# Four image layers with selective scans: the product with B as a TensorE matmul against a diagonal matrix, and the share of C products on GpSimd

## The chip, the cores and the metric

The kernel runs on one core of a Trainium2 chip. The metric is device microseconds of one execution, the median of three runs; lower is better. Besides, one execution was taken by the hardware profiler, and its trace is what is read here.

## The reference

The input is a batch of 4 images of 64 x 64 positions with 192 channels, fp32. Four layers follow one another, each of the form x + layer(groupnorm(x)). All four hold a selective scan over positions with 16 states per channel. Layer a runs four scans (rows and columns, forward and backward) with weights of their own over single rows or columns of 64; layer b one scan over a snake of 4,096 positions; layers c (192 channels) and d (384 channels) four scans over 4,096 positions. The core of each, cut:

```python
x_dbl = einsum('bkdl,kcd->bkcl', xs, x_proj)          # 12 + 16 + 16 rows: dt, B, C
delta = softplus(einsum('bkrl,kdr->bkdl', dts, dt_w) + bias)
A = -exp(A_logs)
def step(h, inp):
    d, bm, cm, uu = inp
    dA = exp(d[..., None] * A[None])
    dBu = (d * uu)[..., None] * bm[:, :, None, :]      # delta*x times B
    h = dA * h + dBu
    y = einsum('bkdn,bkn->bkd', h, cm)                 # sum over the states with C
    return (h, y)
ys = scan(step, h0, ...) + xs * D
```

Ahead of it stand a projection, a short convolution and silu; behind it a sum over directions, a layer norm (not in a), a gate and a projection.

## The kernel before

Images are worked one after another, and in each the layers a, b, c, d. A layer has three stages: projection and convolution, the scans (`scans`), and the output. The four scans of c are packed two by two (`ways` = 2: rows on partitions 0 to 63, columns on 64 to 127), so c has 2 passes, a and d 4, b 1.

A pass of `scans` goes through 4,096 positions in 8 chunks of T = 512. With 32 + 8 + 16 + 32 chunks per image there are 352 in all: 128 in a, 32 in b, 64 in c, 128 in d. A chunk has 24 tiles: 8 groups j of NT = 2 states, and in each 3 blocks b of 128 channels. A tile is [128 channels, 2 states, 512 positions]. For one tile:

- `decay` (L582): two exponentials on ScalarE give dA. Plain tiles put it in a PSUM buffer (tag `ps`, two buffers) and zero the starts with L584; the "turned" tiles put it in one of three fixed SBUF tiles.
- the inflow, delta\*x times B. In half of the groups (j = 0, 2, 4, 6) GpSimd multiplies du by a B broadcast to all partitions by DMA (`inflow`, L588; L593 adds what the carry brings). In the other half (`TURNED`) du is turned once per chunk by TensorE to positions x channels (L504, copied by ScalarE at L511); B is turned too (L490, L497), so that in the turned layout it is a scalar per partition; ScalarE scales the turned du by it (`scaled`, L602, 32 calls a chunk, 64 shorter ones in c), and TensorE turns the result back into a PSUM buffer of tag `ps` (`turned_inflow`, L611, 8 transposes a tile; in b, c and d L618 adds the carry's part as a small matmul).
- `scan` (L633): one VectorE scan. It writes to SBUF (`h`, four buffers) if GpSimd does the C product, else over its input in PSUM.
- `outflow` (L648): h times the broadcast C, on GpSimd or VectorE as the string `PRODUCTS` says; before, 15 of 24 tiles on GpSimd ("p") and 9 on VectorE ("d"). `save_carry` keeps the last column (ScalarE L639 or VectorE L641).
- `total` (L688): 8 transposes into an accumulating PSUM bank sum over the states and turn the result; L679 adds the skip term x\*D as a matmul against a diagonal matrix, L695 the sum of the directions before; `store` (L702, L706) writes it out.

The next chunk's preparation is spread over a chunk's steps by the table `at`: x is loaded at step 0, projected at 3 to 5 (L413), copied to `dbl` and stored to DRAM as `bc` at 6 (L420, L424), delta is made at 7 to 12 (L430, L438, L442), du at 13 (L485), turned at 15 to 20.

The order on each engine is the program's own: `keep` ties every instruction to the one before it on its engine. A step s issues the decay and turned inflow of the coming tiles, the scan of tile s, C products of s or s - 1, and the sum of s - 1 (VectorE product) or s - 3 (GpSimd product). All DMAs go through SyncE's one queue, with B ordered six steps ahead of its tile and C three. What a tile waits for on another engine is found by buffer dependencies.

Of the kernel before, what the change touches and what calls it, by code (L numbers as in the profile page):

```python
# [7 lines left out]
F32 = mybir.dt.float32  # L8
AF = mybir.ActivationFunctionType
# [9 lines left out]
T = 512  # L19
# [6 lines left out]

TURNED = 1, 3, 5, 7
CONV_ROWS = 16
CONV_SPLIT = 37

PRODUCTS = "dpdpppdpdpppdddpppdpdppp"
SUM_AT = 12
# [14 lines left out]
class Net:  # L47
    def __init__(self, tc, d, const):
        self.tc, self.nc, self.d = tc, tc.nc, d
        self.pinned, self.const = {}, const  # L50
        nc = self.nc
        self.ident = const.tile([128, 128], F32, tag="ident", name="ident")
        make_identity(nc, self.ident)
        self.gmat = const.tile([HP, HP], F32, tag="gmat", name="gmat")
        nc.sync.dma_start(self.gmat, d["gmat"])

    @contextmanager
# [234 lines left out]
    def scans(self, sp, pp, dp, xc, P, nb, dirs, short):  # L292
# [23 lines left out]
        XR = ways * (DR + 2 * NS)  # L316
        half = nb * P // 2
        width = W if short else T
        zeros = sp.tile([P, NT, T // width], F32, tag="zeros", bufs=1, name=f"zeros_{dirs[0][3]}")
# [4 lines left out]
            sp.tile([P, NT, T], F32, tag=f"dAs{k}", bufs=1, name=f"dAs{k}_{dirs[0][3]}")  # L324
            for k in range(3)
        ]
        senses = [None] * 3

# [54 lines left out]
        def p_dir(c):  # L383
            prev = chunks[c.n - 1].o if c.n else None
            c.new = not prev or chunks[c.n - 1].i != c.i
            c.o = direction(c.i) if c.new else prev
            c.B, c.C, c.py, c.scaled = {}, {}, {}, {}
# [30 lines left out]
        def p_dbl(c):  # L418
            c.dbl = sp.tile([XR, T], F32, tag="dbl", bufs=1, name=f"dbl_{c.key}")
            keep(nc.scalar.copy(c.dbl, c.px))  # L420
            c.bc = dp.tile([ways, 2 * NS, T], F32, tag="bc", bufs=3, name=f"bc_{c.key}")
            for g in range(ways):
                k = g * (DR + 2 * NS) + DR
                keep(nc.sync.dma_start(c.bc[g], c.dbl[k : k + 2 * NS, :]))  # L424
            c.delta = sp.tile([P, nb, T], F32, tag="delta", bufs=2, name=f"delta_{c.key}")

# [59 lines left out]

        def p_turn_B(c):
            c.tb = spare(c, [128, TB, XR], f"tb_{c.key}")
            for q in range(TB):
                keep(nc.tensor.transpose(  # L490
                    c.tb[:, q, :], c.dbl[:, q * 128 : (q + 1) * 128], self.ident[:XR, :XR]
                ))

        def p_BT(c):
            c.BT = sp.tile([128, TB, ways, NS], F32, tag="BT", bufs=2, name=f"BT_{c.key}")
            tb = c.tb.rearrange("p q (g r) -> p q g r", g=ways)
            keep(nc.scalar.copy(c.BT, tb[:, :, :, DR : DR + NS]))  # L497
            c.duT = sp.tile([128, TB, nb * P], F32, tag="duT", bufs=2, name=f"duT_{c.key}")

        def p_turn_du(b):  # L500
            def f(c):
                c.td = spare(c, [128, TB, P], f"td_{c.key}{b}")
                for q in range(TB):
                    keep(nc.tensor.transpose(  # L504
                        c.td[:, q, :], c.du[:, b, q * 128 : (q + 1) * 128], self.ident[:P, :P]
                    ))
            return f

        def p_duT(b):
            def f(c):  # L510
                keep(nc.scalar.copy(c.duT[:, :, b * P : (b + 1) * P], c.td))  # L511
            return f
# [7 lines left out]
            7: [p_pd(0)], 8: [p_pre(0)], 9: [p_pd(1)], 10: [p_pre(1), p_pd(2)], 11: [p_pre(2)],  # L520
            12: [p_softplus, p_turn_B], 13: [p_du, p_BT, p_first],
        }
# [12 lines left out]
        def load_B(t):  # L535
            t.c.B[t.j] = broadcast(t.c, "B", t.j, t.j * NT, 2)

        def load_C(t):
            t.c.C[t.j] = broadcast(t.c, "C", t.j, NS + t.j * NT, 3)
# [6 lines left out]
        for n, c in enumerate(chunks):  # L546
            c.n = n
            for j in range(NS // NT):
                for b in range(nb):
                    t = Tile()  # L550
                    t.c, t.b, t.j, t.n0 = c, b, j, j * NT
                    t.turned = j in TURNED
                    t.turn = turns
                    turns += t.turned
                    t.starts = b == 0
                    t.pool_c = PRODUCTS[len(tiles) % per_chunk] == "p"
                    t.key = f"{c.key}_{t.n0}{b}"
                    tiles.append(t)
# [4 lines left out]
        def decay(t):  # L563
            c, o = t.c, t.c.o
            if t.turned:
                t.dA = fixed[t.turn % 3]
# [6 lines left out]
            if t.turned and senses[t.turn % 3] != o.rev:  # L573
                keep(nc.scalar.copy(starts, zeros if short else zeros[:, 0]))
                senses[t.turn % 3] = o.rev
            inner = slice(0, width - 1) if o.rev else slice(1, width)
# [17 lines left out]

        def scaled(c, n, q):
            if q == 0:
                c.scaled[n] = sp.tile(
                    [128, TB, nb * P], F32, tag="dut", bufs=3, name=f"dut_{c.key}_{n}"
                )
            o, i = (x[:, q, :].rearrange("p (b g c) -> p b g c", b=nb, g=ways) for x in (c.scaled[n], c.duT))  # L600
            for g in range(ways):
                keep(nc.scalar.activation(  # L602
                    o[:, :, g, :], i[:, :, g, :], AF.Copy, scale=c.BT[:, q, g, n : n + 1]
                ))

        def turned_inflow(t):
            t.u = pp.tile([P, NT, T], F32, tag="ps", bufs=2, name=f"ut_{t.key}")
            for n in (second(t.c), 1 - second(t.c)):
                added = not short and n == second(t.c)
                for q in range(TB):  # L610
                    keep(nc.tensor.matmul(  # L611
                        t.u[:, n, q * 128 : (q + 1) * 128],
                        t.c.scaled[t.n0 + n][:, q, t.b * P : (t.b + 1) * P], self.ident,
                        start=q == 0, stop=q == TB - 1 and not added, is_transpose=True,
                    ))
# [7 lines left out]
        def scan(t):  # L623
            o = t.c.o
            t.h = t.u if t.turned else t.dA
            if t.pool_c:
                t.h = sp.tile([P, NT, T], F32, tag="h", bufs=4, name=f"h_{t.key}")
            af, uf, hf = (x.rearrange("p n t -> p (n t)") for x in (t.dA, t.u, t.h))
# [79 lines left out]

        scales = {}
        for k, t in enumerate(tiles):  # L710
            if t.turned and t.b == 0:
                ops = [(t.c, t.n0 + n, q) for n in range(NT) for q in range(TB)]
                steps = range(k - 2 * nb, k - 1)
                for i, op in enumerate(ops):
                    scales.setdefault(max(steps[i * len(steps) // len(ops)], -1), []).append(op)

        N = len(tiles)
        for f in [f for k in sorted(at) for f in at[k]]:
            f(chunks[0])
        for t in tiles[:6]:  # L720
            if t.starts and not t.turned:
                load_B(t)
        for t in tiles[:3]:
            if t.starts:
                load_C(t)
        decay(tiles[0])
        for t in tiles[:3]:
            if not t.turned:
                inflow(t)
        for op in scales.get(-1, []):  # L730
            scaled(*op)
        for s in range(N + 5):
            t = tiles[s] if s < N else None
            if s + 1 < N and not tiles[s + 1].turned:
                decay(tiles[s + 1])
            if s + 2 < N and tiles[s + 2].turned:
                decay(tiles[s + 2])
            if s + 1 < N and tiles[s + 1].turned:
                turned_inflow(tiles[s + 1])
            for op in scales.get(s, []):  # L740
                scaled(*op)
            if t:
# [3 lines left out]
            if 2 <= s < N + 2 and tiles[s - 2].pool_c and not short:  # L746
                save_carry(tiles[s - 2])
            if s + 6 < N and tiles[s + 6].starts and not tiles[s + 6].turned:
                load_B(tiles[s + 6])
            if s + 3 < N and tiles[s + 3].starts:  # L750
# [309 lines left out]
def net(tc, d):  # L1060
    layers = "abcd"
    with tc.tile_pool(name="const", bufs=1) as const, tc.tile_pool(
# [3 lines left out]
        st = n.new_moments("x")  # L1066
        with tc.tile_pool(name="first", bufs=1) as pool:
            for ch in range(NCH):
# [102 lines left out]
```

## Time and profile before

| | |
|---|---|
| median of 3 runs | 30,964.6 us (30,964.6 to 30,968.0) |
| span of the profiled execution | 30,966.4 us |
| mean granted TensorE clock | 0.869 |
| DMA | 3,330.6 MB, mean 108 GB/s, 34.8% of 16 engines |

How to read it: a busy time counts an engine's work over the span, with overlapping matmuls counted once. PE is the matmul side of TensorE, PEld its weight loads, DVE is VectorE, ACT ScalarE, POOL GpSimd, SP SyncE. A group of instructions has its line, its output and inputs, shapes and count, busy time and mean duration in ns. Timeline rows have start, duration, engine, line and count. Matmuls overlap, so the mean duration of one is longer than the distance between two; that distance is read from the starts of weight loads. Some groups:

| line | what | engine | count | mean |
|---|---|---|---|---|
| L633 | scan, layer a / d | DVE | 1,536 / 1,536 | 2.27 / 2.34 us |
| L648 | C product | POOL | 1,920 in a | 2.37 us |
| L648 | C product | DVE | 1,152 in a | 1.22 us |
| L588 | B product | POOL | 1,536 in a | 2.38 us |
| L602 | scaling of turned du | ACT | 4,096 in a | 0.61 us |
| L611 | turning back | PE | 12,288 in a | 0.30 us |
| L688 | sum over states | PE | 24,576 in a | 0.31 us |

### The profile page before, as it was taken

How to read it: one execution, taken by the hardware profiler on the slowest of the kernel's cores; microseconds unless marked ns; L12 is line 12 of the kernel's file. 1: busy time of each engine (PE TensorE's matmuls, PEld its weight loads, DVE VectorE, ACT ScalarE, POOL GpSimd, SP SyncE). 2: the span in 40 equal slices, each digit the busy share in tenths (PEclk: the TensorE clock that was granted, in tenths of full speed). 3: DMA queues.
4: the chain of work that ended last, by engine and by line, in shares of the span. 5: the costliest groups of instructions: out<-in, count | busy, mean ns of one | idle time of the engine just before them, and what ended most of it. 6: DMA issues, size and time to landing. Idle time of an engine off the chain costs nothing. (4 is left out here: it accounts for less than half of the span.)

```text
span 30966.4 us, 377424 instructions
## 1 busy us (share of the span) xinstructions
PE 23496.1 (76%) x134728; PEld 17601.4 (57%) x134728; DVE 26106.5 (84%) x17436; ACT 23185.8 (75%) x45261; POOL 24377.8 (79%) x13726
## 2 busy tenths in 40 slices
PE   7778777777777877777777787777777778777777
PEld 4664565665466456566546645656655664565665
DVE  8995788998899578899889957889988995788998
ACT  7883686887788368688778836868877883696887
POOL 5992696998599269699869926969986992696998
PEclk8889888888888888888888898888888889888888
DMA  3332343333333234333333323433333332343333
GB/s 116 117 118 81 98 113 104 104 113 114 113 117 118 80 99 113 103 104 113 114 113 118 118 80 99 114 103 104 111 115 115 117 116 81 100 114 101 105 111 112
DMA packets 1371014, 3330.55 MB, mean 108 GB/s; under 512 B 187576, under 2 KB 635432, under 8 KB 1361448
## 3 DMA queue, kind: packets, MB, share of 16 engines
q1 hardware_dynamic: 1369128, 3306.40, 34.8%
q8 instruction: 1063, 17.42, 0.2%
q14 instruction: 823, 6.74, 0.1%
HBM read 2825.66 MB, written 480.25 MB: 107 GB/s over the span
## 5 line engine op out<-in xcount | busy, mean ns | idle before, releaser
L688 PE MATMUL py_d<-ident,c_d 128*128 128x128 f32 x24576 | 3853.0, 313 | 1636.6 <-DVE c_d L648 1106.2
L688 PE MATMUL py_a<-ident,c_a 128*128 128x128 f32 x24576 | 3723.2, 308 | 1616.7 <-DVE c_a L648 1304.1
L648 POOL TENSOR_TENSOR c_a<-h_a,C_a 128x1024 f32<-128x1024 f32 x1920 | 4511.3, 2368 | 330.5 <-DVE h_a L633 296.0
L648 POOL TENSOR_TENSOR c_d<-h_d,C_d 128x1024 f32<-128x1024 f32 x1920 | 4507.1, 2362 | 165.2 <-issue 128.9
L688 PEld LDWEIGHTS py_d<-ident,c_d 128*128 128x128 f32 x24576 | 3326.5, 163 | 2184.6 <-DVE c_d L648 1060.9
L688 PEld LDWEIGHTS py_a<-ident,c_a 128*128 128x128 f32 x24576 | 3251.7, 160 | 1972.9 <-DVE c_a L648 1413.3
L633 DVE TENSOR_TENSOR_SCAN h_d<-dAs_d,carry_d,ut_d 128x1024 f32<-128x1024 f32 x1536 | 3546.9, 2336 | 404.4 <-PE ut_d L611 264.8
L588 POOL TENSOR_TENSOR u_d<-du_d,B_d 128x1024 f32<-128x1024 f32 x1536 | 3643.7, 2372 | 0.0
L588 POOL TENSOR_TENSOR u_a<-du_a,B_a 128x1024 f32<-128x1024 f32 x1536 | 3622.3, 2376 | 0.3
L633 DVE TENSOR_TENSOR_SCAN h_a<-dAs_a,ut_a 128x1024 f32<-128x1024 f32 x1536 | 3430.6, 2273 | 227.6 <-PE ut_a L611 215.4
L633 DVE TENSOR_TENSOR_SCAN dA_d<-dA_d,carry_d,u_d 128x1024 f32<-128x1024 f32 x1152 | 2692.7, 2337 | 298.6 <-ACT dA_d L584 298.2
L633 DVE TENSOR_TENSOR_SCAN dA_a<-dA_a,u_a 128x1024 f32<-128x1024 f32 x1152 | 2623.0, 2277 | 381.1 <-ACT dA_a L584 381.1
L582 ACT ACTIVATE dA_d<-delta_d,A_d 128x512 f32<-128x512 f32 (+1 forms) x3072 | 2122.7, 691 | 952.6 <-DVE h_d L633 697.8
L582 ACT ACTIVATE dA_a<-delta_a,A_a 128x512 f32<-128x512 f32 x3072 | 2124.0, 691 | 828.9 <-DVE h_a L633 593.7
L688 PE MATMUL py_c<-ident,c_c 128*128 128x128 f32 x12288 | 1909.7, 312 | 936.0 <-DVE c_c L648 689.8
L611 PE MATMUL ut_d<-ident,dut_d 128*128 128x128 f32 x12288 | 2101.5, 297 | 378.5 <-ACT dut_d L602 272.7
L648 POOL TENSOR_TENSOR c_c<-h_c,C_c 128x1024 f32<-128x1024 f32 x960 | 2253.2, 2362 | 154.2 <-issue 106.5
L611 PE MATMUL ut_a<-ident,dut_a 128*128 128x128 f32 x12288 | 1888.3, 299 | 614.3 <-ACT dut_a L602 349.0
L602 ACT ACTIVATE dut_d<-duT_d,BT_d 128x384 f32<-128x384 f32 x4096 | 2316.8, 606 | 0.0
L688 PEld LDWEIGHTS py_c<-ident,c_c 128*128 128x128 f32 x12288 | 1661.9, 163 | 1142.3 <-DVE c_c L648 672.3
L602 ACT ACTIVATE dut_a<-duT_a,BT_a 128x384 f32<-128x384 f32 x4096 | 2293.2, 605 | 0.3
L611 PEld LDWEIGHTS ut_d<-ident,dut_d 128*128 128x128 f32 x12288 | 1603.3, 162 | 1001.5 <-issue 388.2
(379 smaller groups left out, 57835.9 us busy)
## 6 DMA issues: line engine op xcount, KB each, us to landing
C_a<-bc_a SPq DMA_DIRECT2D x1024, 512.0 KB
C_d<-bc_d SPq DMA_DIRECT2D x1024, 512.0 KB
B_a<-bc_a SPq DMA_DIRECT2D x512, 512.0 KB
C_c<-bc_c SPq DMA_DIRECT2D x1024, 256.0 KB
B_d<-bc_d SPq DMA_DIRECT2D x512, 512.0 KB
C_b<-bc_b SPq DMA_DIRECT2D x256, 512.0 KB
B_c<-bc_c SPq DMA_DIRECT2D x512, 256.0 KB
xd_a<-xo_a SPq DMA_DIRECT2D x48, 2048.0 KB
```

The costliest lines, as they stand in the source:

```text
L582: keep(nc.scalar.activation(out, delta, AF.Exp, scale=o.A[:, t.b, k : k + 1]))
L588: keep(nc.gpsimd.tensor_tensor(t.u, t.c.du[:, t.b, None, :].to_broadcast([P, NT, T]), t.c.B[t.j], ALU.mult))
L602: keep(nc.scalar.activation(o[:, :, g, :], i[:, :, g, :], AF.Copy, scale=c.BT[:, q, g, n : n + 1]))
L611: keep(nc.tensor.matmul(t.u[:, n, q * 128 : (q + 1) * 128], t.c.scaled[t.n0 + n][:, q, t.b * P : (t.b + 1) * P], self.ident, start=q == 0, ...
L633: keep(nc.vector.tensor_tensor_scan(hf, af, uf, initial, ALU.mult, ALU.add))
L648: keep(engine.tensor_tensor(t.cm, t.h, t.c.C[t.j], ALU.mult))
L688: keep(nc.tensor.matmul(c.py[b][:, q, :], t.cm[:, n, q * 128 : (q + 1) * 128], self.ident[:P, :P], start=first, stop=last and q == TB - 1 ...
```

## The change

ScalarE's scaling goes. Instead, for each group of 2 states the kernel has a matrix D in SBUF: for each piece of 128 positions (64 in c) a diagonal matrix with B on its diagonal. The turned du is the stationary operand and D the moving one, so that one matmul multiplies by B and turns back.

The diagonals come from DRAM. At the program's start four DRAM images of [128, 9216] (two for the plain layers, two for c) are written with zeros. For every chunk a DMA scatters the 16 rows of B from `dbl`, element by element, to the diagonals (row step `ROW + 1`), into one image of two in turn; `load_D` then loads 128 x 1024 elements per group, six steps ahead of its tile, into one of three buffers. Between chunks the zeros stay.

In a, b and d all eight groups work so, and no B is loaded; in c six of eight (j = 0, 1, 3, 4, 6, 7). In c the two halves of the partitions hold different B, so the turned du is laid out in two tiles that are zeroed once, with 8 pieces of 64 positions for the two halves; the copy after turning is four copies in place of one. TensorE's L611 is then 8 true matmuls per tile (16 in c) in place of 8 transposes.

GpSimd gets 22 of 24 C products in a, b and d and 18 of 24 in c. There are four fixed decay tiles in place of three and five `h` buffers in place of four, and a turned tile's decay is ordered three steps ahead, not two. The turning and copying of B (L490, L497) go.

```diff
-TURNED = 1, 3, 5, 7
+DIAGONAL = {1: tuple(range(8)), 2: (0, 1, 3, 4, 6, 7)}
+ROW = 9216
-PRODUCTS = "dpdpppdpdpppdddpppdpdppp"
+PRODUCTS = {1: "pppdppppppppppdppppppppp", 2: "pdppppddppppppdppddppppp"}
...
+    def diagonals(self, pool, dp):
+        nc = self.nc
+        zero = pool.tile([128, ROW], F32, tag="zero", name="zero")
+        nc.vector.memset(zero, 0.0)
+        self.diag = {}
+        for ways in (1, 2):
+            self.diag[ways] = []
+            for k in range(2):
+                t = dp.tile([128, ROW], F32, tag=f"dg{ways}{k}", bufs=1, name=f"dg{ways}{k}")
+                nc.sync.dma_start(t, zero)
+                self.diag[ways].append(t)
...
+        G = P // ways
+        NQ = T // G
...
-            for k in range(3)
+            for k in range(4)
...
+            c.dg = self.diag[ways][c.n % 2]
+            for g in range(ways):
+                k = g * (DR + 2 * NS) + DR
+                to = bass.AP(
+                    c.dg.tensor, c.dg.offset + g * G * ROW,
+                    [[NT * T // NT, NS], [G, NQ], [ROW + 1, G]],
+                )
+                keep(nc.sync.dma_start(to, c.dbl[k : k + NS, :].rearrange("n (q t) -> n q t", t=G)))
...
-                keep(nc.scalar.copy(c.duT[:, :, b * P : (b + 1) * P], c.td))
+                for g in range(ways):
+                    to = c.duT[g * G : (g + 1) * G, :, b * P + g * G : b * P + (g + 1) * G]
+                    for k in range(ways):
+                        td = c.td[k * G : (k + 1) * G, :, g * G : (g + 1) * G]
+                        keep(nc.scalar.copy(to[:, k::ways, :], td))
...
+        def load_D(t):
+            c = t.c
+            c.D[t.j] = sp.tile([128, NT, NQ, G], F32, tag="D", bufs=3, name=f"D_{c.key}{t.j}")
+            at = t.j * NT * T
+            keep(nc.sync.dma_start(
+                c.D[t.j].rearrange("p n q t -> p (n q t)"), c.dg[:, at : at + NT * T]
+            ))
...
-        def scaled(c, n, q):
...
-                for q in range(TB):
+                for q in range(NQ):
                     keep(nc.tensor.matmul(
-                        t.u[:, n, q * 128 : (q + 1) * 128],
-                        t.c.scaled[t.n0 + n][:, q, t.b * P : (t.b + 1) * P], self.ident,
-                        start=q == 0, stop=q == TB - 1 and not added, is_transpose=True,
+                        t.u[:, n, q * G : (q + 1) * G],
+                        t.c.duT[:, q, t.b * P : (t.b + 1) * P], t.c.D[t.j][:, n, q, :],
+                        start=q == 0, stop=q == NQ - 1 and not added,
                     ))
...
-                t.h = sp.tile([P, NT, T], F32, tag="h", bufs=4, name=f"h_{t.key}")
+                t.h = sp.tile([P, NT, T], F32, tag="h", bufs=5, name=f"h_{t.key}")
...
-            if s + 2 < N and tiles[s + 2].turned:
-                decay(tiles[s + 2])
+            if s + 3 < N and tiles[s + 3].turned:
+                decay(tiles[s + 3])
...
-            for op in scales.get(s, []):
-                scaled(*op)
...
-            if s + 6 < N and tiles[s + 6].starts and not tiles[s + 6].turned:
-                load_B(tiles[s + 6])
+            if s + 6 < N and tiles[s + 6].starts:
+                (load_D if tiles[s + 6].turned else load_B)(tiles[s + 6])
```

More of the change, by code (lines that the diff above doesn't have):

```diff
@@ L324, in scans @@
             sp.tile([P, NT, T], F32, tag=f"dAs{k}", bufs=1, name=f"dAs{k}_{dirs[0][3]}")
-            for k in range(3)
+            for k in range(4)
         ]
-        senses = [None] * 3
+        senses = [None] * 4
+        turned_du = []
+        if ways == 2:
+            for k in range(2):
+                turned_du.append(sp.tile(
+                    [128, NQ, nb * P], F32, tag=f"duT{k}", bufs=1, name=f"duT{k}_{dirs[0][3]}"
+                ))
+                keep(nc.gpsimd.memset(turned_du[k], 0.0))
         def view(t, b, ci, cols):
@@ L386, in p_dir @@
             c.o = direction(c.i) if c.new else prev
-            c.B, c.C, c.py, c.scaled = {}, {}, {}, {}
+            c.B, c.C, c.D, c.py = {}, {}, {}, {}
             c.sums, c.xs = [0] * nb, None
@@ L485, in p_du @@
             keep(nc.gpsimd.tensor_tensor(du, delta, x, ALU.mult))
-        def p_turn_B(c):
-            c.tb = spare(c, [128, TB, XR], f"tb_{c.key}")
-            for q in range(TB):
[L490 to L498, printed above, removed]
         def p_turn_du(b):
             def f(c):
+                if ways == 2:
+                    c.duT = turned_du[c.n % 2]
+                elif b == 0:
+                    c.duT = sp.tile([128, NQ, nb * P], F32, tag="duT", bufs=2, name=f"duT_{c.key}")
                 c.td = spare(c, [128, TB, P], f"td_{c.key}{b}")
@@ L520, in scans @@
             7: [p_pd(0)], 8: [p_pre(0)], 9: [p_pd(1)], 10: [p_pre(1), p_pd(2)], 11: [p_pre(2)],
-            12: [p_softplus, p_turn_B], 13: [p_du, p_BT, p_first],
+            12: [p_softplus], 13: [p_du, p_first],
         }
@@ L536, in load_B @@
             t.c.B[t.j] = broadcast(t.c, "B", t.j, t.j * NT, 2)
+        def load_D(t):
[4 more added lines that the diff above has]
+                c.D[t.j].rearrange("p n q t -> p (n q t)"), c.dg[:, at : at + NT * T]
+            ))
         def load_C(t):
@@ L551, in scans @@
                     t.c, t.b, t.j, t.n0 = c, b, j, j * NT
-                    t.turned = j in TURNED
+                    t.turned = j in DIAGONAL[ways]
                     t.turn = turns
@@ L555, in scans @@
                     t.starts = b == 0
-                    t.pool_c = PRODUCTS[len(tiles) % per_chunk] == "p"
+                    t.pool_c = PRODUCTS[ways][len(tiles) % per_chunk] == "p"
                     t.key = f"{c.key}_{t.n0}{b}"
@@ L565, in decay @@
             if t.turned:
-                t.dA = fixed[t.turn % 3]
+                t.dA = fixed[t.turn % 4]
             else:
@@ L572, in decay @@
                 starts = starts[:, second(c)]
-            if t.turned and senses[t.turn % 3] != o.rev:
+            if t.turned and senses[t.turn % 4] != o.rev:
                 keep(nc.scalar.copy(starts, zeros if short else zeros[:, 0]))
-                senses[t.turn % 3] = o.rev
+                senses[t.turn % 4] = o.rev
             inner = slice(0, width - 1) if o.rev else slice(1, width)
@@ L593, in inflow @@
                 keep(nc.gpsimd.tensor_tensor(u, u, t.c.f[:, t.j, t.b : t.b + 1], ALU.add))
-        def scaled(c, n, q):
[L596 to L604, printed above, removed]
         def turned_inflow(t):
@@ L609, in turned_inflow @@
                 added = not short and n == second(t.c)
-                for q in range(TB):
+                for q in range(NQ):
                     keep(nc.tensor.matmul(
-                        t.u[:, n, q * 128 : (q + 1) * 128],
-                        t.c.scaled[t.n0 + n][:, q, t.b * P : (t.b + 1) * P], self.ident,
-                        start=q == 0, stop=q == TB - 1 and not added, is_transpose=True,
+                        t.u[:, n, q * G : (q + 1) * G],
+                        t.c.duT[:, q, t.b * P : (t.b + 1) * P], t.c.D[t.j][:, n, q, :],
+                        start=q == 0, stop=q == NQ - 1 and not added,
                     ))
@@ L706, in store @@
                 keep(nc.sync.dma_start(far, near))
[L709 to L715, printed above, removed]
         N = len(tiles)
@@ L720, in scans @@
         for t in tiles[:6]:
-            if t.starts and not t.turned:
-                load_B(t)
+            if t.starts:
+                load_D(t) if t.turned else load_B(t)
         for t in tiles[:3]:
@@ L725, in scans @@
                 load_C(t)
-        decay(tiles[0])
+        for t in tiles[:3]:
+            if t.turned:
+                decay(t)
+        if not tiles[0].turned:
+            decay(tiles[0])
+        else:
+            turned_inflow(tiles[0])
         for t in tiles[:3]:
@@ L729, in scans @@
                 inflow(t)
-        for op in scales.get(-1, []):
-            scaled(*op)
         for s in range(N + 5):
@@ L735, in scans @@
                 decay(tiles[s + 1])
-            if s + 2 < N and tiles[s + 2].turned:
-                decay(tiles[s + 2])
+            if s + 3 < N and tiles[s + 3].turned:
+                decay(tiles[s + 3])
             if s + 1 < N and tiles[s + 1].turned:
                 turned_inflow(tiles[s + 1])
-            for op in scales.get(s, []):
-                scaled(*op)
             if t:
@@ L1067, in net @@
         with tc.tile_pool(name="first", bufs=1) as pool:
+            n.diagonals(pool, dp)
             for ch in range(NCH):
```

## The prediction

> **What bounds the kernel now.** I read the busy line of the page first, then single chunks of the scan through the table of engines by stretch, then the same stretches for one line of code at a time, then the timeline.
>
> ```profile
> PE 23496.1 (76%) x134728; PEld 17601.4 (57%) x134728; DVE 26106.5 (84%) x17436; ACT 23185.8 (75%) x45261; POOL 24377.8 (79%) x13726
> ```
>
> No engine is over 84%, but this is a mean over scans and the stages between them. A chunk of a scan runs from one softplus (L442) to the next; in the timeline these starts lie 68.1 us apart in layer a, 71.6 in b, 71.7 in c, 71.5 in d. One chunk each of a, c and d (columns: stretch, length, busy PE, PEld, DVE, ACT, POOL with counts, clock, DMA share, GB/s):
>
> ```profile
> 896.50:964.50 68.00, 50.98 (x342) 42.37 (x340) 64.01 (x34) 59.43 (x108) 66.21 (x29) 0.87 0.35 118
> 4097.80:4169.50 71.70, 52.82 (x364) 45.47 (x364) 66.12 (x43) 66.34 (x155) 68.89 (x44) 0.88 0.41 112
> 6006.10:6078.20 72.10, 56.00 (x347) 43.03 (x346) 66.31 (x43) 60.83 (x122) 69.73 (x45) 0.88 0.35 111
> ```
>
> POOL is busy for 66.2 of 68.0 us and DVE for 64.0: these two hold the chunk together. PE has room, and part of its time is at half clock. A chunk has 24 steps, so a step takes 2.84 us in a and 2.98 in d.
>
> **What leaves POOL, DVE and ACT.** In a, b and d all 12 POOL inflow products (L588, 2.37 us) go, and 7 C products move from DVE (L648, 1.22 us) to POOL (2.36 us): 15 of 24 become 22. POOL in a becomes 22 x 2.368 + 3.5 (du, L485) = 55.6 us, in d 22 x 2.362 + 3.8 + 0.3 (small products of the carry) = 56.1. DVE in a becomes 24 x 2.276 (scan) + 2 x 1.224 = 57.1, in d 24 x 2.337 + 2 x 1.215 + 2 x 0.16 (L641) = 58.8. ACT loses L602, 17.9 us of its 59.4 in a. In c (18 products on POOL, 6 inflows left) POOL has 18 x 2.362 + 6 x 2.37 + 3.4 (L485) + 6 x 0.19 (L593) = 61.3 and DVE 24 x 2.337 + 6 x 1.22 + 6 x 0.16 = 64.4. If nothing else moved, a chunk would end near DVE's sum.
>
> **What comes to PE.** The transposes of scaled delta\*x (L611) become true matmuls, and there are twice as many in a, b and d. Two things are needed: how many records a true fp32 matmul makes, and how far apart they start. The diagonal matmul of the skip term (L679) has the new form already: 128x128 stationary data times a moving 128-column diagonal, fp32.
>
> ```profile
> L679 PE MATMUL py_a<-dgD_a,xs_a 128*128 128x128 f32 x3072 | 412.9, 278 | 0.0
> ```
>
> The code calls it 128 chunks x 3 blocks x 4 = 1536 times; the profile has 3072. So a true matmul is two weight loads and two passes, where a transpose (L688: 128 x 24 x 8 = 24576 calls, 24576 records) is one. The distance, from weight loads in the timeline where PE has no gap:
>
> ```profile
> 989.80 0.90 PEld L611 LDWEIGHTS ut_a<-ident,dut_a 128*128 128x128 f32 x8
> 990.68 0.90 PEld L688 LDWEIGHTS py_a<-ident,c_a 128*128 128x128 f32 x8
> 991.58 0.88 PEld L611 LDWEIGHTS ut_a<-ident,dut_a 128*128 128x128 f32 x8
> 992.42 0.90 PEld L688 LDWEIGHTS py_a<-ident,c_a 128*128 128x128 f32 x8
> ```
>
> ```profile
> 928.31 0.97 PEld L679 LDWEIGHTS py_a<-dgD_a,xs_a 128*128 128x128 f32 x8
> 928.42 1.06 PE L679 MATMUL py_a<-dgD_a,xs_a 128*128 128x128 f32 x8
> ```
>
> Eight transposes follow eight others after 0.88 us: 0.11 us each. Eight records of L679 take 0.97 against 0.90: 0.112 each, so 0.224 per matmul. After an idle gap the spacing is twice this (983.41 us: 16 transposes in 3.28 us after 4.83 idle).
>
> A tile's inflow (2 states x 4 pieces x 2 records) is 16 x 0.112 = 1.79 us of PE, its sum over states (L688) 8 x 0.11 = 0.88. Together 2.67 us a step, where DVE's scan needs 2.28 in a and 2.34 elsewhere: **PE becomes the longest engine**. Per chunk of a: inflow 384 x 0.112 = 43.0; L688 192 x 0.11 = 21.1; turning du (L504) 12 x 0.11 = 1.3; skip term (L679) 24 x 0.112 = 2.7; L413 3.0 and L430 3.4 (busy in the stretch above, by line). Sum **74.5 us** against 68.1. L490 (0.44 us) goes.
>
> In b, c, d the carry (L618) adds per turned tile 0.13 us: from 12005.69 to 12006.69 eight transposes and two carry records take 1.00 us, where eight alone take 0.88. So b: 74.5 + 24 x 0.13 = **77.6**. In d, L413 averages 4.2 (2.97 in row directions, 5.50 in column ones), L695 (3.96 in 6006.1:6078.2) stands in three directions of four and L679 in one: 43.0 + 21.1 + 1.3 + 3.1 + 4.2 + 3.4 + 3.0 + 0.7 = **79.8**.
>
> In c a piece has 64 columns, so 18 tiles x 16 pieces x 2 = 576 records. No such row exists. L490 has 44 columns in a and 88 in c behind a 128-column weight load: four records busy 0.44 and 0.47 us, last one 0.235 and 0.24, so 0.068 and 0.077 apart. Bounds: 0.062 (a little under the 44-column value) and 0.112. I take 0.07, between the two nearest rows: 40.3 + 21.1 + 1.3 + 18 x 0.13 + 3.0 + 3.1 + half of 4.0 and of 2.7 = **74.5**.
>
> The Trainium skill speaks harder against this change: "FP8 and Floating Point Precision", section "TensorE Precision Notes", has true fp32 as four passes through the array. By it an inflow would cost 32 records, a chunk of a 74.5 + 43 = 117 us. The trace counts two records and I go by it.
>
> **What lies beside PE.** PE must also not wait. Two PSUM buffers hold inflows, so inflow s+1 waits for scan s-1. PE ends inflow s+1 at T; scan s+1 ends at about T + 2.5; inflow s+3 is due at T + 0.88 + 1.79 + 0.88 = T + 3.55: no wait. Where the product stays on DVE the buffer is free at T + 3.8, 0.3 us late, twice a chunk: I add **0.6 us** to each chunk. POOL's outputs have three buffers and are read three steps later: 2.36 us of work in a step of 3.1. ACT's decays get a fourth buffer and a lead of three steps.
>
> **DMA.** Eight 512 KB loads of D replace four of B in a, b, d (c: six of D for twelve half loads of B): 2 MB more per chunk, at 118 GB/s for a 0.35 share some 6 us of DMA time under 75: hidden, a load has six steps. The scatter writes 16 x 512 single elements on the same queue, between the loads of step 6 and those of step 9. The loads behind it are needed from step 13 on, so about 6.5 steps x 3.1 - 2 = 18 us are free. No row has single-element writes. Below: bc\_d, 64 KB in long rows, is issued at 5300.38 and B is loaded from it at 5302.02, 1.6 us. Above: four loads of dv\_d (L350, 384 single elements each) go from 5293.54 to DVE's use at 5297.18; 3.64 us / 1536 x 8192 = 19.4 us. I take 12, toward the single-element row, so nothing is left over.
> The Trainium skill ("DMA: Bandwidth & Descriptors", section "Specifications") says transfers under 512 B are read-modify-written. If that doubled the row above it would be some 39 us, 21 beyond the cover, about 7,400 us in all. No run here shows it.
>
> Once: four zero images of 4.7 MB at 337 GB/s (118 / 0.35), ahead of later x loads, 60 us with the memset. At each of 16 scan starts the first inflow now waits for du, its turn and copy: about 6 us, 96 in all.
>
> **Sum.** a: (75.1 - 68.1) x 128 = 896; b: (78.2 - 71.6) x 32 = 211; c: (75.1 - 71.7) x 64 = 218; d: (80.4 - 71.5) x 128 = 1,139; with 156: 2,620. The profiled span is 30,966.4 and the median of the runs 30,964.6, so nothing to correct: **about 33,580 us**, 8.5% slower. The gain on POOL, DVE and ACT is real but lies behind PE.
>
> **Rivals.** (1) *The scatter blocks the queue.* Loads of C and D wait behind it; with 28 us, 10 are uncovered in each of 352 chunks: 37,100; with 24, 35,700. For: no cheap single-element row; against: 9 to 20 us fit.
> (2) *Faster: the two passes overlap.* If records of the inflow start under 0.076 us apart, a's PE sum (31.5 + 384 x 0.076) falls to DVE's 57.1 / 0.94 = 60.7, and chunks end at 60.7, 64, 70, 64 us: 28,900. It wins from 0.094 us down. For: only the idea that one weight serves both passes; against: L679's 0.112.
> (3) *Clock.* At the present mean of 0.87 PE's sums grow by 11 us a chunk: 37,500. Against: half clock follows idle gaps, which vanish.
> (4) *c at 0.112 us*: 24 us more in 64 chunks, 35,100.
>
> **Chances.** Forecast 62%, (1) 20%, (2) 5%, (3) 6%, (4) 7%. Without the 0.6 us and with c at 0.062 the sum is some 33,100; the low end, 32,450, lies 1.8 us a chunk below that, for tails of records that busy times count twice; the high end, 36,000, takes in (4) and the milder half of (1). Left out: (2), (3), the rest of (1). The measurement resolves about 0.2%: faster 0.05, within 0.01, slower 0.94.
>
> **What would show it.** In a steady chunk of a: 626 PE records, clock near 1.0, PE busy over 95%, POOL near 56 and DVE near 57 us, DVE waiting for PE ut. Wrong if DVE or PE waits for DMA D or C after the scatter (1), if inflow records lie under 0.1 us apart (2), or at 0.21 (3).

## The result, and the profile after

The changed kernel takes 36,901.8 us (median of 4 runs, 36,884.9 to 36,919.5); the kernel before took 30,966.3 us in the runs beside it. The ratio is 1.192, 95% interval 1.190 to 1.193. The forecast was 33,580 with 36,000 as its high end: the direction was right, the size short by 3,320 us.

The busy line of the page after. TensorE is at 94%, every other engine has fallen, as the forecast had it. There are 251,592 PE records against 134,728.

```profile
PE 34518.8 (94%) x251592; PEld 29581.2 (80%) x251592; DVE 23824.5 (65%) x13917; ACT 16768.8 (45%) x29679; POOL 20407.7 (55%) x9798
```

One chunk each of a, b, c and d in the table of engines by stretch (columns as before: stretch, length, busy PE, PEld, DVE, ACT, POOL with counts, clock, DMA share, GB/s):

```profile
964.20:1039.80 75.60, 75.34 (x626) 69.36 (x625) 56.97 (x27) 40.91 (x63) 55.38 (x24) 1.00 0.57 134
3604.50:3685.40 80.90, 80.74 (x675) 74.76 (x674) 58.65 (x29) 43.16 (x85) 55.83 (x27) 1.00 0.53 114
4953.90:5077.70 123.80, 112.99 (x855) 107.89 (x854) 63.69 (x36) 46.73 (x97) 61.09 (x34) 0.86 0.55 83
6966.00:7049.30 83.30, 83.14 (x697) 77.16 (x696) 60.27 (x29) 45.43 (x89) 58.22 (x28) 1.00 0.52 113
```

In a, b and d PE is busy for all but 0.2 to 0.3 us of a chunk and the clock is full. The third row is another picture: 123.8 us, and neither is PE busy throughout nor is its clock full. Chunk by chunk (distance from one softplus to the next, now L474):

| scan | before, median | before, mean | forecast | after, median | after, mean | forecast growth | growth of the mean | miss x chunks |
|---|---|---|---|---|---|---|---|---|
| a | 68.2 | 68.0 | 75.1 | 75.6 | 74.9 | 7.0 | 6.9 | -10 |
| b | 71.7 | 68.9 | 78.2 | 80.9 | 77.6 | 6.6 | 8.7 | +70 |
| c | 71.7 | 70.4 | 75.1 | 123.8 | 122.2 | 3.4 | 51.7 | +3,090 |
| d | 71.5 | 70.8 | 80.4 | 80.9 | 81.3 | 8.9 | 10.5 | +200 |

The mean takes in the shorter first chunks of a pass, which the forecast did not set apart; so growth is compared with growth, and the last column is their difference x 128, 32, 64, 128. Outside these chunks the kernel grew by 100 us, where the forecast had 156. The packed double scan c holds over nine tenths of the miss. Three views of c say what happens there. First the weight loads of the inflow in a and in c, PE without a gap and the clock full:

```profile
987.19 1.87 PEld L635 LDWEIGHTS ut_a<-D_a,duT_a 128*128 128x128 f32 x16
988.98 0.91 PEld L712 LDWEIGHTS py_a<-ident,c_a 128*128 128x128 f32 x8
```

```profile
5030.59 1.86 PEld L635 LDWEIGHTS ut_c<-D_c,duT_c 128*128 128x128 f32 x16
5032.38 0.30 PEld L642 LDWEIGHTS ut_c<-f_c,ident 128*128 128x128 f32 x2
5032.60 1.87 PEld L635 LDWEIGHTS ut_c<-D_c,duT_c 128*128 128x128 f32 x16
```

Sixteen records of a, with 128 moving columns, take 988.98 - 987.19 = 1.79 us; sixteen of c, with 64, take 5032.38 - 5030.59 = 1.79 us as well: 0.112 each. The two carry records, with one moving column, take 0.22 us: 0.11 each. All three have the same weight load, 128 columns of fp32. Second, SyncE's queue and GpSimd in a chunk of c:

```profile
4930.52 8.63 SPq L456 DMA_DIRECT2D dg<-dbl_c  x2
4939.19 13.73 SPq L559 DMA_DIRECT2D B_c<-bc_c  x2
```

```profile
4960.84 2.35 POOL L623 TENSOR_TENSOR u_c<-du_c,B_c 128x1024 f32<-128x1024 f32 x1 [9.67 <-DMA B_c<-bc_c]
```

In c a chunk has two scatters (x2), one for each half of the partitions. Behind them the issue of the two half loads of B alone takes 13.73 us, and GpSimd, which still makes the inflow of groups 2 and 5 in c, waits 9.67 us for that B. Third, PE in the steps that follow:

```profile
4970.70 1.97 PE L712 MATMUL py_c<-ident,c_c 128*128 128x128 f32 x8 [0.98 <-POOL c_c L672]
4974.09 1.12 PE L527 MATMUL td_c<-ident,du_c 128*128 128x128 f32 x4 [1.42 <-POOL du_c L517]
4979.19 1.97 PE L712 MATMUL py_c<-ident,c_c 128*128 128x128 f32 x8 [3.98 <-POOL c_c L672]
4980.95 3.51 PE L635 MATMUL ut_c<-D_c,duT_c 128*128 128x64 f32 x16
4998.68 1.90 PE L635 MATMUL ut_c<-D_c,duT_c 128*128 128x64 f32 x16
```

PE waits for GpSimd's late products, its clock halves at 4970.5, and sixteen records that took 1.79 us now take 3.3 to 3.4, until the clock is full again at 4997.8. Two stretches of this chunk, 28 us with part at half clock and 20 after it:

```profile
4982.00:5010.00 28.00, 28.00 (x187) 28.00 (x187) 11.95 (x9) 10.86 (x25) 6.64 (x4) 0.72 0.24 65
5010.00:5030.00 20.00, 20.00 (x183) 20.00 (x183) 11.71 (x7) 7.67 (x16) 10.67 (x5) 1.00 0.42 115
```

Both are busy from end to end; the first does 187 records in 28 us, the second 183 in 20. Busy time alone would not tell them apart.

### The profile page after: what moved, and what is told of

The parts are those of the page before. It is cut to its first block, busy times and chain, and to the rows that moved or that the text cites. A ratio compares the mean times of both kernels' runs of the same rounds, so it can differ in the third digit from the quotient of the medians.

```text
span 36887.3 us, 599295 instructions
## 1 busy us (share of the span) xinstructions
PE 34518.8 (94%) x251592; PEld 29581.2 (80%) x251592; DVE 23824.5 (65%) x13917; ACT 16768.8 (45%) x29679; POOL 20407.7 (55%) x9798
## 3 DMA queue, kind: packets, MB, share of 16 engines
q1 hardware_dynamic: 4984936, 4077.21, 52.7%
## 5 line engine op out<-in xcount | busy, mean ns | idle before, releaser
L657 DVE TENSOR_TENSOR_SCAN h_d<-dAs_d,carry_d,ut_d 128x1024 f32<-128x1024 f32 x2816 | 6591.6, 2345 | 2823.9 <-PE ut_d L635 2191.6
L657 DVE TENSOR_TENSOR_SCAN h_a<-dAs_a,ut_a 128x1024 f32<-128x1024 f32 x2816 | 6412.9, 2284 | 2366.6 <-PE ut_a L635 1995.1
L635 PE MATMUL ut_d<-D_d,duT_d 128*128 128x128 f32 x49152 | 6748.0, 282 | 24.9 <-DVE c_d L672 21.3
L635 PEld LDWEIGHTS ut_d<-D_d,duT_d 128*128 128x128 f32 x49152 | 5992.1, 192 | 937.4 <-issue 635.8
L635 PEld LDWEIGHTS ut_a<-D_a,duT_a 128*128 128x128 f32 x49152 | 5723.7, 192 | 657.4 <-issue 487.6
L635 PE MATMUL ut_a<-D_a,duT_a 128*128 128x128 f32 x49152 | 6062.5, 277 | 37.1 <-DVE c_a L672 33.2
L617 ACT ACTIVATE dAs_a<-delta_a,A_a 128x504 f32<-128x504 f32 x6144 | 4045.2, 708 | 3275.7 <-DVE h_a L657 3005.6
L617 ACT ACTIVATE dAs_d<-delta_d,A_d 128x512 f32<-128x512 f32 (+1 forms) x6144 | 4091.8, 714 | 2963.6 <-DVE h_d L657 2897.8
L635 PE MATMUL ut_c<-D_c,duT_c 128*128 128x64 f32 x36864 | 4948.4, 294 | 86.9 <-DMA D_c<-dg 43.0
L635 PEld LDWEIGHTS ut_c<-D_c,duT_c 128*128 128x128 f32 x36864 | 4814.3, 211 | 266.4 <-issue 130.0
```

What stands on the lines that cost most here:

```text
L617: keep(nc.scalar.activation(out, delta, AF.Exp, scale=o.A[:, t.b, k : k + 1]))
L635: keep(nc.tensor.matmul(t.u[:, n, q * G : (q + 1) * G], t.c.duT[:, q, t.b * P : (t.b + 1) * P], t.c.D[t.j][:, n, q, :], start=q == 0, stop ...
L657: keep(nc.vector.tensor_tensor_scan(hf, af, uf, initial, ALU.mult, ALU.add))
```

## Experiments

The theory at this point: in c a record costs what its weight load costs, 0.112 us with half the columns, and the two scatters hold back B, which costs PE idle time and then clock. The rival: one of the two is the whole of it. All runs are of one execution with a profile unless an interval is given; the kernel before took 30,958 to 30,966 us beside them.

**Half the records in c** (each with two pieces of the matrix as one; leaves out half of the products' terms).

```diff
-                for q in range(NQ):
+                for q in range(0, NQ, ways):
                     keep(nc.tensor.matmul(
-                        t.u[:, n, q * G : (q + 1) * G],
-                        t.c.duT[:, q, t.b * P : (t.b + 1) * P], t.c.D[t.j][:, n, q, :],
+                        t.u[:, n, q * G : (q + ways) * G],
+                        t.c.duT[:, q, t.b * P : (t.b + 1) * P],
+                        t.c.D[t.j][:, n, q : q + ways, :].rearrange("p q t -> p (q t)"),
```

> Layer c only: the inflow takes half of the pieces, each with 128 moving columns in place of 64 (its stationary half of the positions is used for both, so c's product with B is not the reference's): 288 records per chunk in place of 576, the same columns streamed. Theory A, a true fp32 matmul pays for its 128-column weight load, 0.1115 us a record whatever the columns: c's inflow falls from 64 to 32 us of PE at full clock, a chunk of c from 124 to between 75 and 92 us (the scatters stay and have less cover), in all 33,700 to 34,850 us. Theory B, a record costs by its moving columns (0.07 at 64, 0.112 at 128) and c is slow from the scatters and the clock alone: PE falls by 8 us, a chunk to about 115, in all some 36,350.

35,179.8 us: 1,722 less, between the two expectations. A chunk of c is 96.3 us on average. The records' price did not change with their columns, in the weight loads of this run:

```profile
4942.67 0.97 PEld L635 LDWEIGHTS ut_c<-D_c,duT_c 128*128 128x128 f32 x8
4943.56 0.30 PEld L643 LDWEIGHTS ut_c<-f_c,ident 128*128 128x128 f32 x2
```

Eight records with 128 columns in 0.89 us: 0.111 each. The mean chunk falls by 25.8 us. What keeps this under 288 x 0.111 = 32 us is that PE is no longer the bound. In this run it waits behind B and GpSimd:

```profile
4905.56 3.68 PE L713 MATMUL py_c<-ident,c_c 128*128 128x128 f32 x16 [14.75 <-POOL c_c L673]
```

**No scatter in c** (the matrices of c stay empty, so six groups of eight have no inflow there).

```diff
-            for g in range(ways):
+            for g in range(ways if ways == 1 else 0):
                 k = g * (DR + 2 * NS) + DR
```

> Layer c only: its two scatters per chunk are left out, so its D stays zero and the product with B is missing in the turned tiles; all other work stays. Theory A (c is 99 us of PE at full clock, and the rest of 124 us is B and C waiting behind two scatters of 15 us each, and the half clock that follows): a chunk of c is 99 to 102 us, PE at full clock in c, in all about 35,350 us. Rival, the half clock and the waits come from the order of the steps in c and not from the scatters: a chunk stays over 118 us, in all over 36,500.

35,957.8 us: 944 less, between the two expectations: a chunk of c is 107.7 us on average, 14.4 less in place of the 24 expected. Two chunks of it:

```profile
4844.90:4950.40 105.50, 99.06 (x855) 94.81 (x854) 63.70 (x36) 46.75 (x97) 61.15 (x34) 1.00 0.35 97
4950.40:5067.40 117.00, 110.49 (x855) 106.24 (x854) 63.77 (x37) 46.89 (x97) 61.59 (x36) 0.90 0.33 90
```

The first has no half clock at all and gives the price of c on PE: 99.06 us of work (855 records; 24 us above the 75 of the forecast) and 6.4 us of gaps in two places, most of it before sums whose C products come late (2.09 and 1.75 us for products on VectorE, 1.28 for one on GpSimd). The expectation had left those gaps out. In the second the gaps are the same to 0.1 us, but here the clock halves after them, for 17.1 and 6.8 us, and the chunk is 11.5 us longer. B is no longer waited for. Beside the first of the two, the chunk of the change shown above has 4.4 us more of gaps and 13.9 more of busy time for the same 855 records: most of what the scatters cost there is clock.

**Both at once**, the two edits above together; with the empty matrices six groups of c have no inflow.

> Two edits in the double scan at once: half the records, each with 128 moving columns where the change has 64, and no scatter of B. Both leave work out. Theory: the miss is the sum of two things, records whose price does not fall with their columns (99.1 us of TensorE a chunk at full clock) and the two scatters, which hold back B, leave TensorE idle for some 11 us and so half its clock. With both gone TensorE has 99.1 - 288 x 0.1115 = 67 us, 6.5 us of gaps remain as in the run without scatters: 73 to 80 us a chunk, 33,600 to 34,100 us in all, about what the forecast said of the whole change. Rival: a third cause (the order of the steps, the transfers of the diagonal matrices) holds the chunk: over 88 us, more than 34,600.

34,091.9 us, at the upper end. A chunk of c:

```profile
4767.00:4847.70 80.70, 69.95 (x566) 65.24 (x565) 63.46 (x37) 46.66 (x96) 61.49 (x37) 0.96 0.47 130
```

Its mean is 79.3 us. By the forecast's growth of 3.4 the mean would have been 73.8, so the miss of 48.3 us a chunk is made up: 79.3 - 73.8 = 5.5 for what is left with both causes gone, 107.7 - 79.3 = 28.4 for the records, 122.2 - 107.7 = 14.4 for the scatters. Taken in the other order it is 25.8 for the records and 17.0 for the scatters. Neither is the whole, and the rival falls. The split is good to some 3 us: in two runs further down, whose edits leave c alone, its mean is 119.5 (old split of products in a, b, d) and 123.5 (no scatter in a, b, d). That the empty matrices make c faster by their zeros, and not by the missing scatters, has two figures against it: with empty matrices the chunks of a, b and d do not change, and c with full matrices comes down to the same 105.6 us in the next run.

**B ordered earlier in c** (nine steps ahead of its tile, and so ahead of the scatters; nothing left out; the loads ahead of the first step are moved in the same way).

```diff
-            if s + 6 < N and tiles[s + 6].starts:
+            if s + 6 < N and tiles[s + 6].starts and (tiles[s + 6].turned or ways == 1):
                 (load_D if tiles[s + 6].turned else load_B)(tiles[s + 6])
+            if ways == 2 and s + 9 < N and tiles[s + 9].starts and not tiles[s + 9].turned:
+                load_B(tiles[s + 9])
```

> Layer c only: the loads of B are ordered nine steps ahead of their tile, not six, so the load for j = 5 stands ahead of the scatters and not behind them. If GpSimd's wait for this B (9.7 us in the chunk looked at) is the first link of the chain to the idle PE and the half clock: a chunk of c 100 to 108 us, in all 35,350 to 35,900. If the loads of C and D behind the scatters are late as well, the wait only moves to them: a chunk stays within 5 us of 124, in all 36,600 to 36,900.

36,303.2 us, between the two. Of 60 chunks 33 still take over 115 us (55 in the change); in the first pass long and short ones alternate:

```profile
4548.40:4668.90 120.50, 111.28 (x855) 106.98 (x854) 63.70 (x36) 46.73 (x97) 61.16 (x34) 0.89 0.66 86
4442.80:4548.40 105.60, 99.03 (x854) 94.78 (x854) 63.70 (x36) 46.72 (x96) 61.17 (x34) 1.00 0.66 97
```

GpSimd's wait for B is gone from the list of waits. The 105.6 us are those of the run without scatters: in these chunks, with B in time, the scatters cost nothing. In the longer ones TensorE waits 4.44 us for a product of GpSimd behind the turning of du, where it is 1.42 in the short ones:

```profile
4570.31 1.97 PE L712 MATMUL py_c<-ident,c_c 128*128 128x128 f32 x8 [4.44 <-POOL c_c L672]
4461.35 1.09 PE L712 MATMUL py_c<-ident,c_c 128*128 128x128 f32 x8 [1.42 <-POOL c_c L672]
```

The clock halves for 27 us, and 15 us are lost. So of the 14.4 us of the scatters 8.6 came through the late B; the mean, 113.6 us, is 5.8 above that without scatters. In the long chunk GpSimd had itself waited 3.49 us for TensorE just before du, in the short one it had not; why this comes back in some chunks stays open.

**The scatters of c on ScalarE's queue.**

```diff
-                keep(nc.sync.dma_start(to, c.dbl[k : k + NS, :].rearrange("n (q t) -> n q t", t=G)))
+                queue = nc.scalar if ways == 2 else nc.sync
+                keep(queue.dma_start(to, c.dbl[k : k + NS, :].rearrange("n (q t) -> n q t", t=G)))
```

> Layer c only: the two scatters per chunk are issued from ScalarE's DMA queue in place of SyncE's; all else as after. If the loads wait because they stand behind the scatter in SyncE's queue, this acts like leaving the scatters out: a chunk of c 99 to 103 us, in all 35,300 to 35,600. If they wait because the 16 DMA engines are busy with 16,384 single elements whatever the queue, the gain is small: a chunk 112 to 124 us, 36,100 to 36,900. ScalarE is busy for 47 of 124 us, so the issue itself should cost nothing.

37,173.7 us, ratio to before 1.201 (1.197 to 1.204): slower than the change by some 270 us, which neither side expected. The reason stands in the timeline of ScalarE and VectorE (ACTq is ScalarE's DMA issue):

```profile
4816.97 12.23 ACTq L457 DMA_DIRECT2D dg<-dbl_c  x2
4829.24 1.41 ACT L618 ACTIVATE dA_c<-delta_c,A_c 128x512 f32<-128x512 f32 x2 [12.31 <-issue]
4830.95 2.35 DVE L658 TENSOR_TENSOR_SCAN h_c<-dA_c,carry_c,u_c 128x1024 f32<-128x1024 f32 x1 [10.31 <-ACT dA_c L620]
```

Issuing two scatters of single elements holds ScalarE for 12 us. On SyncE that delays other loads; on ScalarE it stops the decays, and VectorE's scan with them. The Trainium skill, "DMA: Bandwidth & Descriptors", section "Issuing engines are not separate DMA queues", says that transfers from any issuing engine share the same DMA engines, and that another issuer saves only the time of issuing, usually small. Here that time is 12 us, and it is what decides.

**c as before, the rest changed** (the scaled scheme and the old split in c only; the edit puts the removed code back for `ways == 2`). Its core:

```diff
-                    t.turned = j in DIAGONAL[ways]
+                    t.turned = j in (TURNED if old else DIAGONAL[ways])
...
+                    if old:
+                        keep(nc.tensor.matmul(
+                            t.u[:, n, q * G : (q + 1) * G],
+                            t.c.scaled[t.n0 + n][:, q, t.b * P : (t.b + 1) * P], self.ident,
+                            start=q == 0, stop=q == NQ - 1 and not added, is_transpose=True,
+                        ))
+                        continue
```

> The double scan (c) makes its products as the kernel before did (four of eight groups turned and scaled, C products split 15 to 9); the other three scans keep the change. Theory: everything that the forecast missed sits in the 64 chunks of the double scan, 124 us each against 71.7 in the kernel before. Then 36,900 - 64 x (124.2 - 71.7) = 33,540 us, less some 70 us that pass between the double scan and the scan behind it: 33,430 to 33,600. Rival: the change also costs something outside those chunks that the chunk distances do not show (table switches, transfers that run over into the next scan): over 33,900.

33,462.8 us, as expected. A chunk of c is 71.7 us again, those of a, b, d stay at 75.6, 80.9 and 80.9. The forecast without its 218 us for c is 33,362, so the rest of the change misses by some 100 us: 3,220 of the 3,320 lie in the double scan and what follows from it.

**No scatter in a, b, d** (their matrices stay empty, so they have no inflow; c keeps its scatters).

```diff
-            for g in range(ways):
+            for g in range(ways if ways == 2 else 0):
```

> The scatter of B left out in the three single scans (so their products are those of empty matrices), kept twice a chunk in the double scan. Theory: one scatter of 15.3 us fits into the some 18 us before the next loads are needed, so it costs a single scan nothing: the changed kernel's 36,900 us within 100, and chunks of 75.6, 80.9 and 83.3 us. Rival: it delays the loads behind it by a few us that hide in the spacing of the chunks; then 1 to 3 us in each of 288 chunks, 36,000 to 36,600.

36,952.4 us (2 runs), as expected; the median chunks of a, b and d are 75.6, 80.9 and 80.9 as in the change (those of d are 80.9 or 83.3 in both): one scatter a chunk is hidden. The issues to landing of the scatters in the change (columns: issues, KB, median us):

```profile
dg<-dbl_a SPq DMA_DIRECT2D x128, 32.0 KB, 15.3
dg<-dbl_c SPq DMA_DIRECT2D x128, 32.0 KB, 14.9
```

**The old split of C products in a, b, d** (15 on GpSimd and 9 on VectorE).

```diff
-PRODUCTS = {1: "pppdppppppppppdppppppppp", 2: "pdppppddppppppdppddppppp"}
+PRODUCTS = {1: "dpdpppdpdpppdddpppdpdppp", 2: "pdppppddppppppdppddppppp"}
```

> As the changed kernel, but in the single scans 15 C products of 24 go to GpSimd and 9 to VectorE, as before. Theory: TensorE is the bound of the single scans (75.34 of 75.60 us busy in a chunk), so which engine makes the C products is worth nothing: VectorE goes from 57.0 to some 66.6 us a chunk and GpSimd falls, both still under 75.6: 36,800 to 37,000 us, 0 to +0.5 us a chunk. Rival: the products that moved to GpSimd are what keeps VectorE's scans on time; then the chunks grow by 2 to 3 us, 288 of them: 37,450 to 37,800.

37,658.9 us: 757 more, the rival's number. A chunk of a is 79.4 us, with VectorE at 65.3:

```profile
950.00:1029.40 79.40, 76.35 (x626) 69.59 (x626) 65.32 (x34) 41.60 (x66) 39.00 (x16) 1.00 0.53 128
```

```profile
970.76 2.02 PE L635 MATMUL ut_a<-D_a,duT_a 128*128 128x128 f32 x16 [0.61 <-DVE c_a L672]
```

PE now waits for a product. Where VectorE makes it, h stands in the PSUM buffer of the inflow, and by the program the inflow after next finds the buffer free one product later. Seven more such tiles cost 3.8 us, 0.54 each. The wait for products is only a part: in this chunk PE waits 1.74 us for them in two places, 1.05 for a decay and 0.25 for a scan, and is busy 1.0 longer for the same 626 records; what ties these to the products was not tried. The prediction's own 0.3 us for each points the same way; the expectation here, made from busy sums, did not use it.

**Mixtures.** Three attempts at a kernel faster than both. First, six groups of eight through the matrix in a, b, d, two on GpSimd, 18 C products on GpSimd, and c as before (one B buffer in place of two in a, b, d, for space):

```diff
-DIAGONAL = {1: tuple(range(8)), 2: (0, 1, 3, 4, 6, 7)}
+DIAGONAL = {1: (0, 1, 3, 4, 6, 7), 2: (0, 1, 3, 4, 6, 7)}
-PRODUCTS = {1: "pppdppppppppppdppppppppp", 2: "pdppppddppppppdppddppppp"}
+PRODUCTS = {1: "pdppppddppppppdppddppppp", 2: "dpdpppdpdpppdddpppdpdppp"}
```

> The change with less of it: in the single scans six groups of eight through the diagonal matrix (0, 1, 3, 4, 6, 7), two on GpSimd (2, 5), 18 C products on GpSimd and 6 on VectorE; the double scan as before. Theory: TensorE is the bound of the single scans by 16 x 0.112 = 1.79 us a tile, so six tiles fewer take 10.8 us from its 75.3: 64.6 in a chunk of the first scan, beside GpSimd 62 and VectorE 62.5; four more products on VectorE, each of which holds a PSUM buffer longer, cost 0.55 us apiece by the run with the old split (3.8 us for 7). So 65 to 68 us against 68.1 before, 71 to 74 against 71.5 in the last scan; in all 30,600 to 31,400. Rival: a chunk of TensorE, GpSimd and VectorE within 3 us of each other runs 5 us over the longest, as in the mixed kernel: 69 to 71 and 76 to 79, 31,500 to 32,200.

34,403.7 us, beyond both. A chunk of a (the median is 79.5), and PE's waits at the first group of GpSimd:

```profile
688.10:768.70 80.60, 69.96 (x530) 62.15 (x528) 61.48 (x30) 42.00 (x67) 59.56 (x25) 0.92 0.52 126
```

```profile
699.28 1.64 PE L729 MATMUL py_a<-ident,c_a 128*128 128x128 f32 x8 [1.17 <-POOL c_a L689]
702.79 1.12 PE L521 MATMUL td_a<-ident,du_a 128*128 128x128 f32 x4 [1.87 <-POOL du_a L513]
707.41 1.97 PE L729 MATMUL py_a<-ident,c_a 128*128 128x128 f32 x8 [3.50 <-POOL c_a L689]
```

While GpSimd makes three inflows and du, PE has no inflow of its own to make and waits for C products behind them; its clock then halves for 14 us. A mean over the chunk hides that the work of each engine comes in blocks. Second, a mixture of three schemes (with three decay tiles, four h buffers, and in a, b, d two buffers each for the matrices and the scaled du and one for B):

```diff
+DIAGONAL = {1: (0, 3, 6), 2: ()}
+SCALED = {1: (1, 4, 7), 2: (1, 3, 5, 7)}
+PRODUCTS = {1: "pppdpdpppppdpddpdppppppp", 2: "dpdpppdpdpppdddpppdpdppp"}
```

> A mix of both schemes, meant to beat both kernels: in the single scans three groups of eight through the diagonal matrix (0, 3, 6), three through scaled and turned delta*x as before (1, 4, 7), two on GpSimd (2, 5); 18 C products on GpSimd and 6 on VectorE; the double scan as before. By the prices measured so far a chunk of the first scan has TensorE 56, VectorE 62.5, GpSimd 62, ScalarE 57 us: some 63 us against 68.1; the others some 66 against 71.5. That is 30,965 - 128 x 5 - 160 x 5.5 + 60 = 29,500 us; 29,200 to 30,400. Rival: with four engines within 10% of each other each waits for the others and TensorE's clock falls with its gaps, as in the kernel before (0.87): no gain, 30,700 to 31,500.

31,914.3 us, ratio 1.031 (1.029 to 1.033): nearer the rival. Chunks of a are 67.1 us (before 68.2), but those of b and d 77 and 79 (before 71.6). Third, this mixture in a alone, with the larger buffers of the change (against the second, the core):

```diff
-        old = ways == 2
+        old = not short
+        mode = 1 if short else 2
```

> The mixed scheme (three groups through the diagonal matrix, three scaled and turned, two on GpSimd; 18 C products on GpSimd) in the first scan alone, with the buffers of the changed kernel; b, c and d as in the kernel before. In the mixed kernel a chunk of the first scan took 67.1 us against 68.2, with fewer buffers. Theory: the mixture pays in that scan, where rows start from nothing and no carry is added: 64.5 to 67.1 us in 128 chunks, less 30 us for two zero images at the start: 30,600 to 30,870 us, ratio 0.988 to 0.997. Rival: what the chunks gain goes to the start and the first chunks of each pass, or the chunk stays at 68: 30,900 to 31,050, a ratio within 0.2% of 1.

31,104.8 us, ratio 1.0046 (1.0033 to 1.0060): a chunk of a is now 69.2 us. Neither expectation held, and why more buffers and an earlier decay make it longer by 2 us stays open. No version beat the kernel before.

## Why the prediction was wrong in size

- **PE as the bound, two records of 0.112 us.** Right. In a the sum was 74.5 and PE is busy for 75.3 of 75.6 us, with 626 records and the clock at 1.00. The Trainium skill's four passes ("FP8 and Floating Point Precision", section "TensorE Precision Notes") would have made 117 us a chunk; the trace shows two.
- **The relief of the others.** Right: POOL 55.6 forecast and 55.4 measured in a, DVE 57.1 and 57.0; in c POOL 61.3 and 61.1, DVE 64.4 and 63.7. None of it shortened anything, but the run with the old split shows that the move of C products was needed: without it 757 us more.
- **The carry at 0.13 us a tile.** Wrong: b has 80.74 - 75.34 = 5.4 us more PE time than a for 24 tiles, 0.225 each, two full records. The stretch of before from which 0.13 came begins behind an idle gap, where the second transpose starts 0.06 us after the first and not 0.11; the eight transposes alone would have taken 0.83 there, not 0.88, so the pair took 0.17. Its two weight loads, of 0.19 us each, take 0.30 together, so they start 0.11 apart already:

```profile
12006.08 0.30 PEld L618 LDWEIGHTS ut_c<-f_c,ident 128*128 128x128 f32 x2
12006.22 0.50 PEld L611 LDWEIGHTS ut_c<-ident,dut_c 128*128 128x128 f32 x4
```

- **c's record at 0.07 us.** This is the step that failed first. The prediction took it "between the two nearest rows", transposes with 44 and 88 moving columns. A true fp32 record with 64 costs 0.112, as with 128 (half the records at 128 columns: 0.111), and as with one (0.11). The end of the bounds at 0.112 was right. The rows to take were those of the same kind of record: L679 with 128 moving columns, and the carry above with one, which was in the trace of before at 0.11. 576 x 0.042 = 24 us a chunk; measured 25.8 to 28.4. The readings of L490 hold (its weight loads start 0.06 us apart in a and 0.08 in c), but they are transposes; why those few start closer together was not tried.
- **The scatter.** 12 us taken, 15.3 measured from issue to landing (its last packet ends 11.4 us after the issue), 18 of cover: right in a, b and d, where it is hidden. In c the step failed by its count: the packets of the two scatters of a chunk run one after the other and end 23.3 us after the first issue, against the same 18, and B for GpSimd, which c alone still loads, stands behind them. 14.4 to 17.0 us a chunk. The doubling to 39 us that the prediction drew from the Trainium skill ("DMA: Bandwidth & Descriptors", section "Specifications") did not come: 15.3 us lies under the row it would have doubled.
- **0.6 us of waits a chunk.** Right in a (0.3 us of 75.6). In c, where GpSimd still makes two groups, PE has 6.4 us of gaps in a chunk even without scatters; the prediction worked out no wait for these groups.
- **Clock.** Full in a, b and d but for the first chunks of a scan, as forecast. In c gaps remain, so half clock does, for 35 us of a chunk on average. The forecast's "half clock follows idle gaps, which vanish" held only where PE is the bound in every step.
- **The rivals.** (4) came true in c and with it (1), in c alone. Each was given its chance by itself, and the range took in only one at a time: 33,580 + 64 x (24 + 17 + 5.5) is 36,556, beyond the high end of 36,000.

## What to carry to other kernels

Price a matmul from a row of the same kind of record and the same stationary width: a true fp32 record behind a weight load of 128 columns cost 0.11 us here with 128, 64 or 1 moving columns, so splitting a matmul of 128 columns into two of 64 doubled it. When a change has a variant for one stage (here the packed scan), count its DMAs, records and who else uses its queue anew for that stage. An engine that becomes the bound must be the bound in every step: each gap costs the gap and then the time at half clock, so look at the chunk in steps before trusting its busy sum.

## What was not expected of the hardware

- Half clock outlasts the gap by far. In the chunk shown PE is busy without a gap from 4979.2 us, and the clock is full only at 4997.8, 18.6 us later; per chunk of c it is half for 35 us on average, mostly 27 to 41, in the one shown for 27.3 and 6.8. The Trainium skill, "TensorE: Matmul & The Clock Gate", section "What's actually happening", gives about 3.4 us of sustained work to return to full clock. The trace's 18.6 us are over five times that, and the measurement decides; what else the gate looks at, no run here tells.
- A scatter of 8,192 single fp32 elements takes 15.3 us from issue to landing. Alone it is issued in 0.6 us, and what is issued behind it is held: in a the next load takes 6.7 us to issue (at 907.11 us), in c the second scatter 8.0 and the B behind it 13.1. On ScalarE two take 12.2.
- Every element is a packet: the hardware queue has 4,984,936 of them after and 1,369,128 before. Packets under 512 B grew by 3,435,072, where the 416 scatters write 3,407,872 elements.
